# Norms beside self-attention: turning a norm one step later, normalizing ahead of the next deviation, and more dummy transposes at the start

## The chip, the cores and the metric

The kernel runs on one core of a Trainium2 chip. The metric is the device time of one execution in microseconds; below 1% this is about small differences, so the median of several runs counts. Beside the times there is a profile of one execution: the span of the core's instructions, and what each engine did in it. The engines are TensorE (PE, and PEld for its weight loads), VectorE (DVE), ScalarE (ACT), GpSimd (POOL) and SyncE (SP), which issues most DMAs.

## The reference

One transformer block in float32: two batches of 1024 tokens with 256 features, 16 heads of 64, a context of 154 tokens with 192 features.

```
h = layernorm(x, ln1);  x = attention(h, h, sa_*) + x
h = layernorm(x, ln2);  x = attention(h, ctx_768, ca_*) + x
h = layernorm(x, ln3);  p = h @ ff_w1 + ff_b1;  a, gate = halves of p
out = a * gelu(gate) @ ff_w2 + ff_b2 + x
```

`attention` projects queries, keys and values, takes softmax(q k / 8) v by head, and multiplies by an output matrix.

## The kernel before

The order of all instructions is written out by hand; each engine runs its own in that order. There are three stages: self-attention (about 20 to 720 us), cross-attention (to about 890 us) and the gated feed-forward part.

**Self-attention** goes over 16 units, a unit being one batch and one pair of heads. A unit has 8 steps (the loop over `p`), and a step handles 128 query rows of the pair's two heads against all 1024 keys. In step `p`:

- `self_first(p)`: TensorE makes scores into two PSUM tiles (line L544, tile `s`), VectorE takes their row maxima (L730), and after that ScalarE takes exponents (L555).
- `flush(stores)` stands between the scores and the exponents: it issues the copies out of PSUM that the step before left behind.
- `join(p - 1)`: the two halves of a row's keys lie on different partitions, so the maxima and sums are exchanged by four small DMAs (tile `st`). GpSimd takes differences (`dd`, L573), ScalarE their exponents (`ee`, L579), GpSimd denominators, VectorE reciprocals (`rd`), and GpSimd scales the exponents' rows (L668).
- `turn_group`: VectorE transposes scaled blocks for the value product (L693).
- Then one piece of other work for TensorE. The last step of each half unit does the first half of the value products (`po`, L596, into both banks of the pool `ps_o`), the first step of the next does the second half. Of the remaining steps, `run_work` fills each with a projection (`pq_sa`, `pk_sa` L387, `pv_sa` L423), or, where no projection is left, with output products (`py_sa`, L518).

`run_work(n, n_side, bank)` first does projections from the queue `work`, `n` banks' worth. It then does `n_side` entries of the queue `side`, then the deferred statistics (`slow`), and then output products from the queue `outs` for the banks that are left.

**Norms** are put into `side` by `norm_beside`, in steps that run beside the attention of other units. `norm_pieces` gives four kinds of pieces. `stats` are VectorE's `bn_stats` and `bn_aggr`. `deviation` is `var` (L265) and `rstd` (L269) on GpSimd. `normalize` is `off` on VectorE (L275) and two instructions that write the normalized tiles, on ScalarE (L294) or on GpSimd (L291). `turn` is four 128x128 transposes on TensorE (L304, tile `ph_ln`) into one bank, whose four copies with gain and shift on ScalarE (L319) or VectorE (L315) are left in `stores`. Which piece goes into which step is set by `lag`. For the narrow norms (ln1 of batch 1 and ln2 of batch 0, both beside self-attention) a step takes one token tile, and otherwise two. `run_work` gives `side` entries to steps 5 and 6 of a unit (counted from 0), so a narrow norm takes six units. A narrow norm's turn falls into step 5, which has a projection, and its normalize into step 6, which has output products.

**The start** (`warm`): while the first inputs are on their way, TensorE transposes the identity matrix (L1304), 12 times, then the context (L221), then 8 times. Next comes the transpose of the first gains and shifts (L1317), which waits for their DMA.

Of the kernel before, what the change touches and what calls it, by code (L numbers as in the profile page):

```python
# [18 lines left out]
def tile_transformer_block(ctx: ExitStack, tc: tile.TileContext, a: dict, out: bass.AP):  # L19
# [12 lines left out]
    NT = S // P  # L32
# [20 lines left out]
    SH = GH // 2  # L53
# [50 lines left out]
    for n in names:  # L104
        k = n_of[n]
# [82 lines left out]
    for n in names[2:]:  # L188
        own = rows[row_of[n] - n_cols:row_of[n] - n_cols + n_of[n], :]
        p = HR if n in twice else P  # L190
# [137 lines left out]
    def tile_order(kind):  # L328

        if kind == "ff":  # L330
            return list(range(NT))
        return [t for i in range(NT // 2) for t in (i, NT // 2 + i)]

    def narrow(kind, b):

        return kind == "sa" or kind == "ca" and b < B - 1

    def add_biases(kind, b):

        bo = {"sa": "sa_bo", "ca": "ca_bo", "ff": "ff_b2"}[kind]  # L340

        def add(t):
            xs = xt[b, t // GT][:, t % GT, :]
            nc.gpsimd.tensor_tensor(xs, xs, bias[bo], ALU.add)

        later.extend(lambda t=t: add(t) for t in range(NT))
        if b == B - 1 and kind != "ff":
            later.append(lambda: load_bias({"sa": "ca_bo", "ca": "ff_b2"}[kind]))

    def norm_beside(kind, b):  # L350

        after = {"sa": None, "ca": "sa", "ff": "ca"}[kind]
        stats, deviation, normalize, turn = norm_pieces(kind, b)
        n = 1 if narrow(kind, b) else 2
        lag = {}
        for fns, first in ((turn, 3), (stats, 0), (deviation, 1), (normalize, 2)):
            for i, fn in enumerate(fns):  # L360
                t = i if fns is stats else 2 * i + 1
                lag.setdefault(first + t // n, []).append((fn, fns is turn))
        for k in range(NT // n + 3):
            tiles = tile_order(kind)[k * n:(k + 1) * n]
            needs = [(after, b, half, t) for half in range(NQ) for t in tiles if after]

            def step(fns=lag[k]):
                slow.extend(fn for fn, _ in fns if fn in stats)
                done = [fn() for fn, _ in fns if fn not in stats]
                return next((fn for fn in done if fn), None)  # L370

            side.append((any(turns for _, turns in lag[k]), needs, step))
        if not narrow(kind, b):
            side.append((False, (), lambda: add_biases(kind, b)))

# [91 lines left out]
    def move_values(b, pr):  # L467

        v = unit_values(b, pr)
        for n in range(2):  # L470
            nc.sync.dma_start(
                out=held_v[n * QG:(n + 1) * QG, 3], in_=v[(1 - n) * QG:(2 - n) * QG])
# [132 lines left out]
    side, lates, slow = [], [], []  # L605
# [3 lines left out]
    def run(piece):  # L609
        done = piece()  # L610
        if done is not None:
            (adds if getattr(done, "adds", False) else stores).append(done)

    def flush(queue):
        for fn in queue:
            fn()
        queue.clear()

    def run_work(n, n_side, bank=None, n_sum=0):

        while n > 0 and work:
            n -= work[0].banks
            run(work.pop(0))
        for _ in range(min(n_side, len(side))):
            needs_bank, needs, fn = side[0]
            if needs_bank and not bank and n <= 0 or not added.issuperset(needs):
                break  # L630
            if needs_bank and not bank:
                n -= 1
            spare["bank"] = bank or mm_tile
            run(fn)
            side.pop(0)
        if not spare["turned"]:
            flush(slow)
        for i in range(min(max(n, 0) + n_sum, len(outs))):
            spare["out"] = mm_tile if i < n else sum_tile
            run(outs.pop(0))  # L640
# [8 lines left out]
    SA = 2 * SH * NU  # L649
# [35 lines left out]
    def turn_group(p, i):  # L685

        if p < 0:
            return
        h, g = divmod(p, SH)
        if g == 0 and i == 0:  # L690
            halves[h] = pt_.tile([P, 2 * NK, QH // 2], F32, tag="pT", name=f"pT_{h}")
        c = (2 * g + i) * KB
        nc.vector.transpose(  # L693
            halves[h][:, :, c:c + KB],
            slots[p]["p"][i].rearrange("p j (n k) -> p (j n) k", k=KB)
        )
# [25 lines left out]
    def self_first(p):  # L722

        b, pr = units[p // (2 * SH)]
        g = p % (2 * SH)
        q, k, _ = qk["sa", b, pr]
        st = small.tile([P, 2, 2, 2, 2], F32, tag="st8", name=f"st_{p}")
        sc = [scores(f"{p}_{i}", q, k, 2 * g + i) for i in range(2)]
        for i in range(2):
            nc.vector.tensor_reduce(st[:, 0, 0, i, :], sc[i], AX.X, ALU.max, negate=True)  # L730
            if i == 0:
                reciprocals(p - 2)

        def then():
            slots[p] = {"st": st, "p": [exponents(f"{p}_{i}", sc[i], st, i) for i in range(2)]}
            join(p - 1)
            exchange(st)

        return then
# [3 lines left out]
    def self_beside(ui):  # L743

        nxt = self_pieces(*units[ui + 1]) if ui + 1 < NU else cross_pieces(*units[0])
        if ui + 1 < NU:
            if ui % 2 == 0 and ui:
                work.append(value_piece(*units[ui], 1))
            work.extend(nxt)
            if ui == 0:  # L750
                work.append(unit_value_piece(*units[1], 0, GT))
            if ui % 2:
                work.append(value_piece(*units[ui + 1], 0))
        else:

            work.extend(nxt[:1])
            held.append(costing(2, lambda: cross_queries(*units[1], KB, tag="KT")))
            held.extend(nxt[1:])
        if ui >= HP:
            ob, og = divmod((ui - HP) // HP, NQ)  # L760
            t0 = (ui % HP) * 2
            out_pieces("sa", ob, og, out_order("sa")[t0:t0 + 2])
        if ui == 1:
            norm_beside("sa", 1)
        if ui in (4, 6):
            add_biases("sa", (ui - 4) // 2)
        if ui == NPAIR + 1:
            norm_beside("ca", 0)
# [507 lines left out]
    with tc.manual_schedule():  # L1276
        stats, deviation, normalize, turn = norm_pieces("sa", 0, True)
        spare["bank"] = sum_tile

        def emit(*pieces):  # L1280
            for piece in pieces:
                run(piece)
            flush(stores)
# [18 lines left out]
        def warm(n):  # L1302
            for _ in range(n):
                nc.tensor.transpose(own[0][:, 1, :P], ident, ident)  # L1304
# [7 lines left out]
        for turned in [turn_context(b) for b in range(B)]:  # L1312
            turned()
        spare["bank"] = sum_tile
        warm(8)
        emit(stats[0], stats[1], deviation[0], stats[2], normalize[0], stats[3], deviation[1])
        nc.tensor.transpose(own[1][:, 1, :n_cols], rows1, ident[:n_cols, :n_cols])  # L1317
        nc.scalar.copy(cols[:, :n_cols], own[1][:, 1, :n_cols])
# [33 lines left out]
        for p in range(SA):  # L1352
            if p % (2 * SH) == 0:
                self_beside(p // (2 * SH))
            if p == SA - SH:
                work.extend(held)
                held.clear()
            then = self_first(p)
            flush(stores)
            then()  # L1360
            turn_group(p - LAG - 1, 1)
            turn_group(p - LAG, 0)
            if adds:
                adds.pop(0)()
            flush(kept)
            if later and (p < 4 or p % (2 * SH) in (2, 4, 6)):
                later.pop(0)()
            if p in ahead:
                ahead[p]()
            load_ahead(p)  # L1370
            h, hg = divmod(p, SH)
            ui, n = divmod(p, 2 * SH)
            if h and hg == SH - 1:
                run(lambda: self_values(h - 1, 0))
            elif h > 1 and hg == 0:
                run(lambda: self_values(h - 2, 1))
            else:
                run_work(2 if p < SA - SH else 1, h % 2 or h == 0, sum_tile)
            if n == SH:
                move_values(*units[ui])  # L1380
            if hg == LAG:
                if n == SH + LAG and ui in (0, 1, NU - 1):

                    pr = {0: 2, 1: 4, NU - 1: 6}[ui]
                    run(lambda: context_keys(pr, sum_tile))
                    kept.append(context_keys(pr + 1, mm_tile))

        for c in range(CA):
# [13 lines left out]
            ui, n = divmod(c, len(CG))  # L1402
# [87 lines left out]
        for k in range(2 * FU):  # L1490
# [18 lines left out]
            while n_left > 0 and sums:  # L1509
                fn, n = sums.pop(0)  # L1510
# [51 lines left out]
```

## Time and profile before

| | |
|---|---|
| Runs | 1063.14, 1064.46, 1069.09 us; median 1064.46 |
| Profiled execution, its own time | 1065.06 us |
| Its span | 1063.3 us (1.8 lie around it) |
| Busy: TensorE, VectorE, GpSimd, ScalarE | 99%, 83%, 72%, 61% |
| DMA | 60.95 MB, mean 57 GB/s |

How to read it: a busy share says how long an engine had something in it, not that it set the time. The chain of waits is followed back from the last instruction and says which engine the end waited for at each moment. The page cuts the span into 40 slices of 26.6 us:

```profile
PE   8999999999999999999999999999999999999998
DVE  4799899998989989999989899979877887565554
ACT  4776677677766666666777766665666554343231
POOL 2677777778777787777777777777766876479984
```

TensorE is busy in nine tenths or more of nearly every slice. VectorE comes close to it in the self-attention stage.

### The profile page before, as it was taken

How to read it: one execution, taken by the hardware profiler on the slowest of the kernel's cores; microseconds unless marked ns; L12 is line 12 of the kernel's file. 1: busy time of each engine (PE TensorE's matmuls, PEld its weight loads, DVE VectorE, ACT ScalarE, POOL GpSimd, SP SyncE). 2: the span in 40 equal slices, each digit the busy share in tenths (PEclk: the TensorE clock that was granted, in tenths of full speed). 3: DMA queues.
4: the chain of work that ended last, by engine and by line, in shares of the span. 5: the costliest groups of instructions: out<-in, count | busy, mean ns of one | idle time of the engine just before them, and what ended most of it. 6: DMA issues, size and time to landing. Idle time of an engine off the chain costs nothing.

```text
span 1063.3 us, 48592 instructions
## 1 busy us (share of the span) xinstructions
PE 1054.3 (99%) x20190; PEld 703.4 (66%) x20190; DVE 883.4 (83%) x1321; ACT 650.5 (61%) x2104; POOL 770.9 (72%) x1644
## 2 busy tenths in 40 slices
PE   8999999999999999999999999999999999999998
PEld 6556657555555556656665655566866667888998
DVE  4799899998989989999989899979877887565554
ACT  4776677677766666666777766665666554343231
POOL 2677777778777787777777777777766876479984
PEclk9999999999999999999999999999999999999999
DMA  4121121131011111111111101116776545000000
GB/s 132 51 61 54 25 73 47 26 69 34 15 45 35 32 44 32 42 34 34 44 34 33 45 14 39 33 51 154 175 181 170 124 99 115 16 10 11 21 10 31
DMA packets 83573, 60.95 MB, mean 57 GB/s; under 512 B 30994, under 2 KB 71898, under 8 KB 83354
## 3 DMA queue, kind: packets, MB, share of 16 engines
q1 hardware_dynamic: 82405, 57.01, 22.3%
q8 instruction: 159, 2.61, 1.0%
q10 hardware_dynamic: 949, 0.84, 0.2%
q14 instruction: 60, 0.49, 0.2%
HBM read 27.91 MB, written 2.10 MB: 28 GB/s over the span
## 4 chain that ended last, share of the span: by engine, by line
PE 93%; DMA 2%; DVE 1%; POOL 1%; ACT 1%; SPq 1%; issue 1%; POOLq 0%; DVEq 0%; ACTq 0%
PE s L544 20%; PE po L596 20%; PE py_sa L518 5%; PE py_ca L518 5%; PE pq_sa L387 5%; PE pk_sa L387 5%; PE pq_ca L387 4%; PE pv_sa L423 4%; PE pb L1084 4%; PE poc L963 4%; PE pq L1229 4%; PE sc L883 3%; PE pa L1084 3%; PE pc L1084 3%; PE pf L1259 1%; PE ph_ln L304 1%
## 5 line engine op out<-in xcount | busy, mean ns | idle before, releaser
L668 POOL TENSOR_SCALAR p<-p,rd,ee 128x512 f32<-128x512 f32 x512 | 390.4, 768 | 88.7 <-DVE rd L658 87.5
L555 ACT ACTIVATE p<-s,st 128x512 f32<-128x512 f32 x512 | 344.9, 686 | 174.6 <-DVE st L730 168.3
L730 DVE TENSOR_REDUCE st<-s 128x2 f32<-128x1024 f32 x256 | 308.6, 1206 | 55.9 <-issue 23.5
L693 DVE STREAM_TRANSPOSE pT<-p 128x1024 f32<-128x1024 f32 x256 | 302.4, 1218 | 0.9 <-POOL p L668 0.9
L544 PE MATMUL s<-k_sa,q_sa 64*32 64x512 f32 x4096 | 255.9, 591 | 0.4 <-ACT p L555 0.4
L596 PE MATMUL po<-pT,held_v 64*32 64x256 f32 x8192 | 237.9, 376 | 0.0
L596 PEld LDWEIGHTS po<-pT,held_v 64*32 64x32 f32 x8192 | 177.1, 106 | 70.3 <-issue 27.8
L544 PEld LDWEIGHTS s<-k_sa,q_sa 64*32 64x32 f32 x4096 | 86.6, 106 | 94.7 <-issue 51.2
L900 ACT ACTIVATE p<-sc,neg 128x154 f32<-128x154 f32 x256 | 96.1, 404 | 74.9 <-DVE rden L908 70.8
L911 POOL TENSOR_SCALAR p<-p,rden 128x154 f32<-128x154 f32 x256 | 96.8, 398 | 47.5 <-DVE rden L908 42.1
L555 ACT ACTIVATION_READ_ACCUMULATOR p<-s,st 128x1 f32 x512 | 103.9, 203 | 0.0
L573 POOL TENSOR_TENSOR dd<-st 128x8 f32<-128x8 f32 x128 | 25.6, 200 | 68.9 <-DMA st<-st 68.3
L518 PE MATMUL py_ca<-ca_wo,o_ca 128*128 128x256 f32 x256 | 60.2, 383 | 0.0
L518 PE MATMUL py_sa<-sa_wo,o_sa 128*128 128x256 f32 x256 | 59.5, 386 | 0.0
L518 PEld LDWEIGHTS py_sa<-sa_wo,o_sa 128*128 128x128 f32 x256 | 47.3, 190 | 17.9 <-issue 5.0
L387 PE MATMUL pq_ca<-hT_ln,ca_wq 64*64 64x512 f32 (+1 forms) x576 | 58.9, 589 | 0.0
L387 PE MATMUL pq_sa<-hT_ln,sa_wq 64*32 64x512 f32 (+1 forms) x976 | 57.7, 587 | 0.7 <-ACT held_v L433 0.7
L889 DVE TENSOR_REDUCE neg<-sc 128x6 f32<-128x924 f32 (+1 forms) x48 | 47.7, 994 | 12.7 <-PE sc L883 12.7
L387 PE MATMUL pk_sa<-hT_ln,sa_wk 64*32 64x512 f32 x960 | 56.7, 590 | 0.0
L900 ACT ACTIVATION_READ_ACCUMULATOR p<-sc,neg 128x1 f32 x256 | 56.4, 220 | 0.0
L927 DVE STREAM_TRANSPOSE pT_ca<-p 128x480 f32<-128x480 f32 (+1 forms) x96 | 52.8, 585 | 0.8 <-POOL p L911 0.6
L518 PEld LDWEIGHTS py_ca<-ca_wo,o_ca 128*128 128x128 f32 x256 | 47.4, 190 | 8.2 <-issue 1.9
(164 smaller groups left out, 1475.4 us busy)
## 6 DMA issues: line engine op xcount, KB each, us to landing
wf<-pT_ca SPq DMA_DIRECT2D x128, 128.0 KB, 2.4
st<-st SPq DMA_DIRECT2D x512, 1.0 KB, 1.7
held_v<-held_v SPq DMA_DIRECT2D x32, 256.0 KB, 3.6
sa_wq<-in_L_xattn_sa_wq_dram SPq DMA_DIRECT2D x32, 128.0 KB, 3.1
sa_wk<-in_L_xattn_sa_wk_dram SPq DMA_DIRECT2D x32, 128.0 KB, 3.2
sa_wv<-in_L_xattn_sa_wv_dram SPq DMA_DIRECT2D x16, 256.0 KB, 4.5
ca_wq<-in_L_xattn_ca_wq_dram SPq DMA_DIRECT2D x32, 128.0 KB, 3.8
wf<-in_L_xattn_ff_w_dram SPq DMA_DIRECT2D x12, 256.0 KB, 4.4
```

What stands on the lines that cost most here:

```text
L387: nc.tensor.matmul(pq[r][f:f + m, at:at + n], lhsT=wt[own, c, f:f + m], rhs=h[own, c, t0:t0 + n], start=(c == 0), stop=(c == NH - 1), tile ...
L518: nc.tensor.matmul(py[:, e * D:(e + 1) * D], lhsT=o[:, i, (t + e) * P:(t + e + 1) * P], rhs=wo[kind][:, g * HP + i, :], start=(i == 0), st ...
L544: nc.tensor.matmul(sc[a4 * KB:(a4 + 1) * KB, j, :], lhsT=q[r, c:c + KB], rhs=k[r, h * HB:(h + 1) * HB], start=True, stop=True, tile_positi ...
L555: nc.scalar.activation(pr[:, j, :], sc[:, j, :], AF.Exp, bias=st[:, 0, 0, i, j:j + 1], accum_out=st[:, 0, 1, i, j:j + 1],)
L596: nc.tensor.matmul(po[a2][d:d + KB, :QH // 2], lhsT=v[e][r, t, d:d + KB], rhs=pT[r, d // DH * NK + n, :], start=(t == 0 and e == 0), stop= ...
L668: nc.gpsimd.tensor_scalar(pr[:, j, :], pr[:, j, :], own["rd"][:, c:c + 1], own["ee"][:, 0, c:c + 1], op0=ALU.mult, op1=ALU.mult,)
L693: nc.vector.transpose(halves[h][:, :, c:c + KB], slots[p]["p"][i].rearrange("p j (n k) -> p (j n) k", k=KB))
L730: nc.vector.tensor_reduce(st[:, 0, 0, i, :], sc[i], AX.X, ALU.max, negate=True)
L900: nc.scalar.activation(pr_[:, j, i, :T], sc[:, j, i * T:(i + 1) * T], AF.Exp, bias=neg[:, j, i:i + 1], accum_out=den[:, j, i:i + 1],)
L911: nc.gpsimd.tensor_scalar(pr_[:, j, i, :T], pr_[:, j, i, :T], rden[:, j, i:i + 1], 1.0, op0=ALU.mult, op1=ALU.mult,)
L927: nc.vector.transpose(pTc["ring"][:, ui % 3, :, j, t0 * KB:(t0 + nt) * KB].rearrange("p n (i q) -> p i n q", q=KB), pr_[:, j, :nt, :].rear ...
L1084: nc.tensor.matmul(into[:, :BT], lhsT=lhs, rhs=wh[pair][i], start=first, stop=True, skip_group_check=True)
```

## The change

1. In `norm_beside`, a turn of a narrow norm comes one entry of `side` later, so in step 6 (with output products) instead of step 5. The wide norms keep their place.
2. Within one entry, `normalize` now stands ahead of `deviation` of the following tiles. This moves something only where both run on GpSimd: ln2 of batch 1 and ln3 of batch 0.
3. In the self-attention loop, `run_work` is called twice: projections, deferred statistics and output products first, and then the entry of `side`. So a turn's transposes stand behind the output products of their step.
4. At the start, `warm(24)` stands for the second `warm(8)`.

In the built program TensorE has the 16 added transposes and the eight narrow turns in their new places. ScalarE has the eight groups of four copies one step later: behind the exponents of step 6, their factors and, in six of the eight, two normalizing activations, and ahead of the exponents of step 7. In each of these step 7s the first product into the second `po` bank has a wait on ScalarE that it did not have before. GpSimd has two normalizing instructions ahead of `var` and `rstd` six times. VectorE's and SyncE's orders stay as they were.

```diff
         lag = {}
-        for fns, first in ((turn, 3), (stats, 0), (deviation, 1), (normalize, 2)):
+        last = 4 if n == 1 else 3
+        for fns, first in ((turn, last), (stats, 0), (normalize, 2), (deviation, 1)):
             for i, fn in enumerate(fns):
                 t = i if fns is stats else 2 * i + 1
                 lag.setdefault(first + t // n, []).append((fn, fns is turn))
-        for k in range(NT // n + 3):
+        for k in range(NT // n + last):
...
-            def step(fns=lag[k]):
+            def step(fns=lag.get(k, [])):
...
-        warm(8)
+        warm(24)
...
             else:
-                run_work(2 if p < SA - SH else 1, h % 2 or h == 0, sum_tile)
+                run_work(2 if p < SA - SH else 1, 0)
+                run_work(0, h % 2 or h == 0, sum_tile)
```

More of the change, by code (lines that the diff above doesn't have):

```diff
@@ L370, in step @@
                 return next((fn for fn in done if fn), None)
-            side.append((any(turns for _, turns in lag[k]), needs, step))
+            side.append((any(turns for _, turns in lag.get(k, [])), needs, step))
         if not narrow(kind, b):
```

## The prediction

> **What bounds the kernel now.** I read the page first, its busy times and the chain that ended last; then the chain in order of time around the places that the change touches; then the waits; then the timeline of one such place, engine by engine.
>
> ```profile
> PE 1054.3 (99%) x20190; PEld 703.4 (66%) x20190; DVE 883.4 (83%) x1321; ACT 650.5 (61%) x2104; POOL 770.9 (72%) x1644
> PE 93%; DMA 2%; DVE 1%; POOL 1%; ACT 1%; SPq 1%; issue 1%; POOLq 0%; DVEq 0%; ACTq 0%
> ```
>
> TensorE is busy for 1054.3 us of the span and carries 93% of the chain. So in the self-attention stage whatever TensorE issues less, or waits more, goes into the time in full, and what VectorE, ScalarE or GpSimd do counts only where TensorE waits for it.
>
> Four transposes that turn a norm ("a turn") stand eight times in that stage: four for ln1 of batch 1 and four for ln2 of batch 0. Here are two units of eight steps in the chain, one with a turn and one without. The columns are start, length, what.
>
> ```profile
> 214.74 3.43 PE pk_sa L387 x64
> 218.18 0.59 PE ph_ln L304 x4
> 218.76 1.88 PE s L544 x32
> 220.64 3.65 PE py_sa L518 x16
> 384.42 3.43 PE pk_sa L387 x64
> 387.85 1.72 PE s L544 x32
> 389.57 3.65 PE py_sa L518 x16
> ```
>
> From the projection (pk) to the output products (py) it takes 220.64 - 214.74 = 5.90 us with the turn and 389.57 - 384.42 = 5.15 without. A turn costs 0.75 where it stands, between narrow tiled products (64x32) on both sides.
>
> **The turn moved: what TensorE saves.** The change takes each turn out of that place, its step 5 of 8, and puts it behind the output products of step 6, which are 128x128 like the transposes. Four transposes in a row cost their own pitch there.
>
> ```profile
> PEld ph_ln L304 <- ACT p L555: 5.0, 8, 0.8
> 389.50 3.32 PEld L518 LDWEIGHTS py_sa<-sa_wo,o_sa 128*128 128x128 f32 x16 [0.84 <-ACT k_sa L410]
> 598.27 0.66 PE L304 MATMUL ph_ln<-ident,hT_ln 128*128 128x128 f32 x4
> 600.74 3.72 PE L518 MATMUL py_sa<-sa_wo,o_sa 128*128 128x256 f32 x16
> 604.39 1.95 PE L544 MATMUL s<-k_sa,q_sa 64*32 64x512 f32 x32
> 606.13 3.66 PE L596 MATMUL po<-pT,held_v 64*32 64x256 f32 x128
> 609.58 1.92 PE L544 MATMUL s<-k_sa,q_sa 64*32 64x512 f32 x32
> L1304 PE MATMUL first<-ident x20: 272/417/473, 1.9 to 6.8; 128*128 128x128 f32 x20
> ```
>
> One transpose lasts 0.27 us (272 ns, the last row's minimum), so four in 0.66 have a pitch of (0.66 - 0.27) / 3 = 0.13, and a turn behind the output products adds 4 x 0.13 = 0.5. Taking away 0.75 and adding 0.5 leaves a gain of 0.25 a turn, 2.0 us over eight. The first row would promise more: the weight loads of the eight turns sat idle for 5.0 us "for ScalarE". I don't count that as a wait. The second row shows the same 0.84 idle before output products that follow narrow products without a turn: it is what the weight path shows at such a change of shape, and the chain's 0.75 holds it already.
>
> **The turn moved: the wait that it brings.** A turn writes into one of the two banks of ps_o, and four ScalarE activations (L319) empty it in the step after. Both banks are taken again by the value products po, at step 7. Now the turn is at step 5, its copies at step 6 and po at step 7. In the changed program the turn is at step 6, and its copies stand in ScalarE's queue in step 7, behind step 6's four exponents, their factors and the next pair's two normalizing activations (L294). The instruction order of the built program shows it: the second bank's first po product has a wait on ScalarE that it didn't have. TensorE issues in order, so all of po and the next scores queue behind it. When are the copies done? The turn of 598:
>
> ```profile
> 599.46 1.54 ACT L319 ACTIVATE hT_ln<-ph_ln,cols 128x128 f32<-128x128 f32 x4
> 600.11 1.22 DVE L730 TENSOR_REDUCE st<-s 128x2 f32<-128x1024 f32 x1 [1.22 <-ACT held_v L433]
> 600.57 0.72 POOL L269 TENSOR_TENSOR rstd_ln<-var_ln,power 128x2 f32<-128x2 f32 x1
> 601.52 1.52 POOL L668 TENSOR_SCALAR p<-p,rd,ee 128x512 f32<-128x512 f32 x2 [0.24 <-DVE rd L658]
> 602.45 2.36 DVE L693 STREAM_TRANSPOSE pT<-p 128x1024 f32<-128x1024 f32 x2
> 604.74 0.12 DVE L275 SCALAR_TENSOR_TENSOR off_ln<-mv_ln,rstd_ln 128x2 f32<-128x2 f32 x1
> 604.89 1.09 ACT L294 ACTIVATE hT_ln<-x,off_ln,rstd_ln 128x256 f32<-128x256 f32 x2 [0.63 <-DVE off_ln L275]
> 606.90 0.69 ACT L555 ACTIVATE p<-s,st 128x512 f32<-128x512 f32 x1 [0.92 <-DVE st L730]
> ```
>
> Normalizing ends at 604.89 + 1.09 = 605.98, 0.15 before po starts (606.13): were ScalarE no earlier than now, the copies would end at 605.9 + 1.54 = 607.4, some 1.3 behind po's present start. It gets earlier, because step 6's scores come 0.75 earlier. VectorE's reduction (600.11) sat idle for 1.22 before them and follows. GpSimd's scaling can't: its rstd ends at 600.57 + 0.72 = 601.29, so scaling starts 0.24 earlier at most and ends at 602.8. The second of VectorE's two block transposes needs it: 602.8 + 1.2 = 604.0, and off comes at 604.05, 0.7 earlier. Normalizing then ends at 605.3, the copies at 605.2 + 1.54 = 606.75. The second bank's po waits until then, though TensorE is there at 606.13 - 0.25 = 605.9. Against now po is late by 606.75 - 606.13 = 0.6, all inclusive. Nothing gives that back: after po the next scores start at once (606.13 + 3.45 = 609.58). The exponents behind the copies lose nothing, they start at 606.90 for VectorE's reduction.
>
> Six of the eight turns share their step with a normalize; I take five of them like this one. The first differs, and of the two without a normalize (the last of each norm) one is shown:
>
> ```profile
> 181.70 0.20 POOL L573 TENSOR_TENSOR dd<-st 128x8 f32<-128x8 f32 x1 [1.09 <-DMA st<-st]
> 182.41 1.08 ACT L294 ACTIVATE hT_ln<-x,off_ln,rstd_ln 128x256 f32<-128x256 f32 x2
> 183.54 1.72 PE L596 MATMUL po<-pT,held_v 64*32 64x256 f32 x56
> 646.46 0.22 ACT L579 ACTIVATE ee<-dd 128x8 f32<-128x8 f32 x1
> 648.55 1.72 PE L596 MATMUL po<-pT,held_v 64*32 64x256 f32 x56
> ```
>
> In the first, ScalarE's factors come behind GpSimd's dd, and that waits for a DMA (181.70) which an earlier TensorE doesn't hasten. Normalizing stays at 182.41, the copies end at 183.4 + 1.54 = 184.95, po is late by 184.95 - 183.54 = 1.4. At 646.46 + 0.22 + 1.54 = 648.2 the copies of the last turn are done before po (648.55 - 0.25 = 648.3): the gain of 0.25 stays. Sum: 5 x 0.6 + 1.4 - 2 x 0.25 = +3.9 us. Bounds for one turn with a normalize: 0.25 won where the copies come in time, 1.4 lost where nothing on ScalarE moves; I take 0.6 because the timeline of the turn at 598 leads there link by link.
>
> **Normalize ahead of the next deviation.** Where GpSimd normalizes (ln2 of batch 1, ln3 of batch 0), two xn instructions now stand ahead of the next var and rstd, six times. Elsewhere the two are on different engines, and no order changes. One of the six is on TensorE's path:
>
> ```profile
> 844.93 0.71 POOL L269 TENSOR_TENSOR rstd_ln<-var_ln,power 128x2 f32<-128x2 f32 x1
> 845.64 1.09 POOL L291 TENSOR_SCALAR xn_ln<-x,rstd_ln,off_ln 128x256 f32<-128x256 f32 x2
> 845.12 0.96 PE L883 MATMUL sc<-kT,q_ca 64*64 64x154 f32 x24
> 846.78 0.55 PE L304 MATMUL ph_ln<-ident,xn_ln 128*128 128x128 f32 x3 [0.21 <-POOL xn_ln L291]
> 847.16 1.68 PE L518 MATMUL py_ca<-ca_wo,o_ca 128*128 128x256 f32 x7
> 859.14 0.79 PE sc L883 x24
> ```
>
> The scores start at 845.12 and take 0.79 on the chain, a turn 0.59, so the output products could start at 846.50; they start at 847.16. With xn ahead by var and rstd, about 1.0, that 0.65 goes. The rstd, later by 1.1, is needed one step on. For the other five I take nothing: the waits name no other of these turns as held by xn. Bounds: 0 to -0.65 here. Taken: -0.6.
>
> **Twenty-four dummies for eight.**
>
> ```profile
> 1.91 2.82 PE L1304 MATMUL first<-ident 128*128 128x128 f32 x12 [1.91 <-POOL ident masks.py:199]
> 6.66 0.38 PE L1304 MATMUL first<-ident 128*128 128x128 f32 x2
> 8.52 0.20 PE L1317 MATMUL first<-ident,held_v 8*128 8x8 f32 x1 [1.47 <-DMA held_v<-in_L_xattn_ln_b_dram]
> ```
>
> TensorE idles for 1.47 until a DMA lets L1317 go. The pitch of the first twelve is (2.82 - 0.47) / 11 = 0.21, that of the last two 0.38 - 0.27 = 0.11: the clock has risen by then, and it outlives the idle time (turns before and after have 0.27 a transpose). Sixteen more at 0.11 are 1.75 us: the last starts near 8.5, and L1317 comes at 8.6 for 8.52. Cost +0.1. The Trainium skill ("TensorE: Matmul & The Clock Gate", Part 4: PE-mode transpose) says that transposes don't bring the clock up, as they don't count as busy the same way; the pitch in these rows speaks against it.
>
> Sum: +3.9 - 0.6 + 0.1 = +3.4 us. The profiled execution took 1065.06, 0.6 above the median of the runs; on the median the sum gives 1064.46 + 3.4 = 1067.9 us. A measurement of this kernel can tell about 0.5%, 5.3 us, from no change, so this lies inside it: no change to speak of, on the slow side. Its own range, with the five at 0.2 to 1.1, is 1065 to 1071.
>
> **Rivals.** *The copies come in time.* ScalarE and VectorE run ahead far enough, po doesn't wait, and the eight turns win 0.25 each: -2.0 - 0.6 + 0.1, 1062.0 us. For it: VectorE does idle ahead of the reduction. Against it: GpSimd's rstd leaves 0.24, and the copies need 1.3. *Every turn pays like the first.* If the DMA of the maxima, or GpSimd, holds ScalarE in all six, po is late by 1.4 each time: 6 x 1.4 - 0.5 - 0.5 = +7.4, 1071.9 us, slower. It decides where step 7's copies start later than po's present start less 0.15. For it: normalizing ends just 0.15 before po now, and the first turn shows such a DMA. Against it: in the turn at 598 the normalize waits 0.63 for VectorE, not for a DMA. *The dummies outlast the idle time.* If the added ones run at 0.21, they take 3.4 from 6.9 to 10.3, and L1317 with the first turn is late by 1.8: 1069.7 us. The page above gives this case by its rule. Against it stands the 0.11 of the last ones. That the change doesn't do what it says I rule out: all three edits show in the instruction order.
>
> **How the numbers follow.** Forecast 0.65, copies in time 0.15, every turn like the first 0.13, dummies 0.07. The range is 1063.0 to 1071.3: it takes in the forecast's own range, leaves out the first rival and the upper part of the second. Slower than 1069.8: a quarter of the forecast, the second rival, half the third, 0.33. Faster than 1059.1 needs more than any step here gives, 0.04. The rest is within 0.5%: 0.63.
>
> **What would show it.** Right: the waits list po behind ScalarE's L319, eight or six times, 0.5 to 1.5 each; ph follows py without idle time; TensorE passes from the scores at 845 to py with no wait for xn; L1317 at 8.5 to 8.7. Wrong: po with no gap at step 7 while step 5 is 0.75 shorter, or L1317 past 9.

## The result, and the profile after

The changed kernel takes 1071.42 us in the median of 12 runs (1068.49 to 1075.21), the kernel before 1066.5 in the median of 12 (1063.14 to 1069.09). The ratio is 1.0045 [1.0032, 1.0059]: slower by 4.8 us, with the interval from 3.4 to 6.3. That is within the 0.5% that the prediction called no change to speak of, on the slow side, though the interval reaches past it. The predicted 1067.9 is 3.5 us too low: 2.0 of that is the base, since 1064.46 was the median of three runs and twelve gave 1066.5, and 1.5 is the change. The median lies 0.1 above the upper end of the range.

The profiled execution of the changed kernel took 1074.59 us, its span 1072.8, one of the longer ones. The page gives busy time and the chain's shares by engine:

```profile
PE 1058.9 (99%) x20206; PEld 735.6 (69%) x20206; DVE 885.4 (83%) x1321; ACT 649.9 (61%) x2104; POOL 773.8 (72%) x1644
PE 78%; DMA 5%; POOL 4%; DVE 4%; SPq 3%; ACT 3%; issue 2%; POOLq 0%; ACTq 0%; DVEq 0%
```

TensorE still looks 99% busy, as before; that number hides the change. The chain doesn't: TensorE's share falls from 93% to 78%, because the path now leaves it for ScalarE and what ScalarE waits for. The waits of the stretch from 165 to 665 us (idle us, times, longest) say where:

```profile
PEld po L597 <- ACT hT_ln L319: 7.3, 8, 1.4
PEld py_sa L519 <- ACT held_v L434: 6.2, 6, 1.6
PE po L597 <- ACT hT_ln L319: 4.0, 6, 0.9
PE py_sa L519 <- ACT held_v L434: 1.1, 2, 0.7
```

Six times the matrix products of po stand still for the turn's copies (L319), and twice the output products for copies of a projection (L434). Lines from L377 on carry a number one higher than before. This is the turn of unit 13, the one that the prediction followed at 598, in the chain in order of time:

```profile
608.28 3.65 PE py_sa L519 x16
611.93 0.44 PE ph_ln L304 x4
612.37 0.24 PE s L545
612.60 0.02 issue
612.63 0.05 ACT hT_ln L294
...
613.13 0.58 ACT hT_ln L294
613.72 1.39 ACT hT_ln L319 x4
615.11 0.04 issue
615.16 3.44 PE po L597 x116
```

The chain goes from TensorE's scores to ScalarE's normalize (L294), on to the copies behind it (L319), and comes back to TensorE with the second bank of po. The timeline has the same place by engine:

```profile
612.63 1.09 ACT L294 ACTIVATE hT_ln<-x,off_ln,rstd_ln 128x256 f32<-128x256 f32 x2 [0.55 <-DVE off_ln L275]
613.63 1.48 ACT L319 ACTIVATE hT_ln<-ph_ln,cols 128x128 f32<-128x128 f32 x4
614.04 0.63 PE L597 MATMUL po<-pT,held_v 64*32 64x256 f32 x8
615.16 3.44 PE L597 MATMUL po<-pT,held_v 64*32 64x256 f32 x116 [0.49 <-ACT hT_ln L319]
```

The first bank's products begin at 614.04 and the second bank's at 615.16, when the copies end (613.63 + 1.48 = 615.11).

To see what that is worth I take the distance from the start of a step's last score product to that of the next step's. The first score products won't do as a mark: they can start while the products before them still run, and some steps have that and others not. Step 6 of unit 5 has it:

```profile
263.66 0.72 PE L545 MATMUL s<-k_sa,q_sa 64*32 64x512 f32 x2
263.85 0.38 PE L424 MATMUL pv_sa<-sa_wv,hT_ln 64*32 64x256 f32 x1
...
264.06 1.90 PE L545 MATMUL s<-k_sa,q_sa 64*32 64x512 f32 x28
```

A turn touches steps 5, 6 and 7 of its unit; these are the sums of the three, in us. The last column adds all eight before rounding. Units 6 and 14 hold the turns without a normalize beside them.

| Kernel | unit 3 | 4 | 5 | 6 | 11 | 12 | 13 | 14 | all |
|---|---|---|---|---|---|---|---|---|---|
| before | 16.62 | 16.60 | 16.62 | 16.60 | 16.62 | 16.60 | 16.62 | 16.60 | 132.9 |
| after | 17.47 | 17.79 | 18.59 | 16.28 | 18.20 | 17.31 | 17.42 | 16.28 | 139.4 |
| copies at once (below) | 16.31 | 16.28 | 16.31 | 16.29 | 16.59 | 16.28 | 16.31 | 16.28 | 130.6 |

By step, the eight units add up to 47.3, 44.2 and 41.4 in steps 5, 6 and 7 before, and to 41.3, 48.9 and 49.2 after. Step 7 takes 5.17 before in each unit; after, it takes 6.19 to 6.67 in the six with a normalize and 5.17 in the two others. The expectations below were written with distances between first score products: there the usual step 7 reads 5.19, and the six long ones 5.84 to 6.32.

Of the 9.5 us between the two profiled spans, 6.5 are in these steps. The rest is spread over other steps: single executions of either kernel differ by 6 us and more, and the profiled one of the changed kernel is 3.2 above its median.

The other two edits behaved as the text said, or nearly. GpSimd's normalize now starts at 854.34, ahead of the next rstd:

```profile
854.34 1.09 POOL L291 TENSOR_SCALAR xn_ln<-x,rstd_ln,off_ln 128x256 f32<-128x256 f32 x2
854.87 0.96 PE L884 MATMUL sc<-kT,q_ca 64*64 64x154 f32 x24
855.76 0.66 PE L304 MATMUL ph_ln<-ident,xn_ln 128*128 128x128 f32 x4
856.25 1.89 PE L519 MATMUL py_ca<-ca_wo,o_ca 128*128 128x256 f32 x8
```

From the scores to the output products it is 856.25 - 854.87 = 1.38 us, against 847.16 - 845.12 = 2.04 before: 0.66 won. At the start the 24 dummies cover the whole idle time:

```profile
5.56 3.46 PE L1305 MATMUL first<-ident 128*128 128x128 f32 x24
8.94 0.22 PE L1318 MATMUL first<-ident,held_v 8*128 8x8 f32 x1
```

The transpose of the first gains comes at 8.94 with no wait, 0.42 later than before (8.52).

### The profile page after: what moved, and what is told of

Same layout as the page of the kernel before. It is cut to its first block, busy times and chain, and to the rows that moved or that the text cites. A ratio compares the mean times of both kernels' runs of the same rounds, so it can differ in the third digit from the quotient of the medians.

```text
span 1072.8 us, 48627 instructions
## 1 busy us (share of the span) xinstructions
PE 1058.9 (99%) x20206; PEld 735.6 (69%) x20206; DVE 885.4 (83%) x1321; ACT 649.9 (61%) x2104; POOL 773.8 (72%) x1644
## 4 chain that ended last, share of the span: by engine, by line
PE 78%; DMA 5%; POOL 4%; DVE 4%; SPq 3%; ACT 3%; issue 2%; POOLq 0%; ACTq 0%; DVEq 0%
PE po L597 17%; PE s L545 14%; PE py_ca L519 5%; DMA st<-st 5%; PE pq_ca L388 5%; PE pq_sa L388 4%; PE pb L1085 4%; PE py_sa L519 4%; PE pk_sa L388 4%; PE poc L964 4%; PE pq L1230 4%; SPq L566 3%; PE pv_sa L424 3%; PE sc L884 3%; PE pa L1085 3%; PE pc L1085 2%
## 5 line engine op out<-in xcount | busy, mean ns | idle before, releaser
L545 PE MATMUL s<-k_sa,q_sa 64*32 64x512 f32 x4096 | 271.6, 590 | 0.6 <-ACT p L556 0.6
L597 PE MATMUL po<-pT,held_v 64*32 64x256 f32 x8192 | 248.8, 376 | 4.4 <-ACT hT_ln L319 4.0
L597 PEld LDWEIGHTS po<-pT,held_v 64*32 64x32 f32 x8192 | 183.1, 106 | 74.1 <-issue 20.3
L545 PEld LDWEIGHTS s<-k_sa,q_sa 64*32 64x32 f32 x4096 | 107.2, 106 | 82.7 <-issue 37.4
L519 PEld LDWEIGHTS py_sa<-sa_wo,o_sa 128*128 128x128 f32 x256 | 47.3, 190 | 19.2 <-ACT held_v L434 6.2
L424 PE MATMUL pv_sa<-sa_wv,hT_ln 64*32 64x256 f32 x1792 | 55.2, 376 | 0.0
```

Of the source, the lines that this page charges most:

```text
L424: nc.tensor.matmul(pv[r][f:f + KB, e * VC:(e + 1) * VC], lhsT=h[half, c, t0:t0 + KB], rhs=wt[half, c, :], start=(c == 0), stop=(c == NH - ...
L519: nc.tensor.matmul(py[:, e * D:(e + 1) * D], lhsT=o[:, i, (t + e) * P:(t + e + 1) * P], rhs=wo[kind][:, g * HP + i, :], start=(i == 0), st ...
L545: nc.tensor.matmul(sc[a4 * KB:(a4 + 1) * KB, j, :], lhsT=q[r, c:c + KB], rhs=k[r, h * HB:(h + 1) * HB], start=True, stop=True, tile_positi ...
L597: nc.tensor.matmul(po[a2][d:d + KB, :QH // 2], lhsT=v[e][r, t, d:d + KB], rhs=pT[r, d // DH * NK + n, :], start=(t == 0 and e == 0), stop= ...
```

## The experiments

Theory A: what the change loses is the wait of po for the turn's copies, which stand on ScalarE behind the normalize. Its rivals stand in the expectations.

**The turn's move alone.** Against the changed kernel:

```diff
-        for fns, first in ((turn, last), (stats, 0), (normalize, 2), (deviation, 1)):
+        for fns, first in ((turn, last), (stats, 0), (deviation, 1), (normalize, 2)):
...
-        warm(24)
+        warm(8)
```

> The kernel before with the turn moved alone (one step later, right behind the output products); normalize stands behind the next deviation and the second group of dummies is 8, as before. Theory A: the time is lost in the wait of the value products po for the turn's copies on ScalarE. Then nearly all of the loss is here: six step 7s of 5.8 to 6.3 us where 5.19 is usual, the waits list names po behind L319 eight times with about 7 us of idle weight loads, and the time is 4 to 6 us over before (ratio 1.0035 to 1.006). Rival B: the sixteen dummies or the order on GpSimd lose it; then this is within 1 us of before.

Measured: 1071.67 us, ratio 1.0052 [1.0033, 1.0072], and PEld's waits of po for L319 are 6.6 us. All of the loss that can be measured is in the turn's move.

**Everything but the turn's move.**

```diff
-        last = 4 if n == 1 else 3
+        last = 3
...
-                run_work(2 if p < SA - SH else 1, 0)
-                run_work(0, h % 2 or h == 0, sum_tile)
+                run_work(2 if p < SA - SH else 1, h % 2 or h == 0, sum_tile)
```

> The changed kernel with the turn back in step 5 and one run_work call; what stays of the change is normalize ahead of the next deviation and 24 dummies for 8. Theory A: the two edits nearly cancel (0.2 to 0.4 lost at the start, 0.5 to 0.65 won at the first turn of ln3), so -0.3 us against before, within the noise. Rival C (the dummies cost more than the profile shows, since they outlast the first DMA): 2 us or more over before.

Measured: 1064.79 us, ratio 0.9992 [0.9979, 1.0006]. The normalize's new order and the dummies together can't be told from nothing.

**The copies at once.** The turn stays where the change puts it, but its four copies are issued in the turn's own step, so on ScalarE they stand ahead of the normalize.

```diff
             def step(fns=lag.get(k, [])):
...
+                if n == 1:
+                    for fn, turns in fns:
+                        if fn not in stats:
+                            done = fn()
+                            if turns:
+                                done()
+                    return None
```

> The changed kernel with one thing different: in the eight narrow turns the four copies out of the turn's bank are issued at once behind its transposes, so that on ScalarE they stand ahead of the two normalizing activations and not behind them. TensorE's order is that of the changed kernel. Theory A: the copies end about 1.1 us earlier, the six long step 7s fall from 5.8-6.3 to 5.2-5.4 us, and the time falls by 3.5 to 5.5 us, to within 2 us of before. Rival B (the place of the transposes behind output products, or output products that wait for the emptying of the projection's banks, loses the time): step 6 stays above 6.2 us, step 7 hardly counts, and the time stays 3 us or more over before.

Measured: 1064.28 us, ratio 0.9982 [0.9971, 0.9993]: faster than both kernels. The waits, and the same turn of unit 13 (lines from there on are seven higher):

```profile
PEld po L604 <- ACT hT_ln L319: 1.4, 7, 0.2
```

```profile
603.02 1.50 ACT L319 ACTIVATE hT_ln<-ph_ln,cols 128x128 f32<-128x128 f32 x4 [0.69 <-PE ph_ln L304]
604.41 1.09 ACT L294 ACTIVATE hT_ln<-x,off_ln,rstd_ln 128x256 f32<-128x256 f32 x2
604.65 3.66 PE L604 MATMUL po<-pT,held_v 64*32 64x256 f32 x128
```

The copies end at 604.52, the normalize comes behind them, and po's 128 products run through in 3.66. Step 7 is back at 5.17 in seven of the eight units, and 5.45 in unit 11 (6.19 to 6.67 in the six turns with a normalize of the changed kernel). The table's last row is 2.2 below the kernel before: the move itself does win about 0.28 a turn, and what the change lost lay in the copies' place in ScalarE's queue.

**The turn ahead of the output products.** In step 6, but not behind them:

```diff
-                run_work(2 if p < SA - SH else 1, 0)
-                run_work(0, h % 2 or h == 0, sum_tile)
+                run_work(2 if p < SA - SH else 1, h % 2 or h == 0, sum_tile)
```

> The changed kernel with run_work called once as before, so that the turn, still in step 6, stands ahead of the output products and not right behind them. ScalarE's order is that of the changed kernel. Theory A: the copies stand at the same place in ScalarE's queue and po waits for them just as long; step 7 stays at 5.8 to 6.3 us and the time within 1 us of the changed kernel's. Rival B (the place right behind the output products is what costs): back to within 1.5 us of before.

Measured: 1071.98 us, ratio 1.0058 [1.0039, 1.0077]. The place beside the output products doesn't matter while po waits. The same edit on top of the copies at once, where po doesn't wait:

> The changed kernel with each narrow turn's copies issued in the turn's own step, and the turn ahead of the output products of step 6 instead of behind them. Theory A: the copies are far ahead of po in both, so no wait for them, ratio 0.997 to 0.999; what is left is the order on TensorE alone: a turn between scores and output products adds what the one behind output products adds, within 0.1 us each, so the two kernels differ by under 1 us. Rival (the place behind the output products is what wins the 0.25 a turn): 1 to 2 us slower than the same with the turn behind them.

Measured: 1063.33 us, ratio 0.9972 [0.9961, 0.9984], its eight units 131.0 in the table's sum, 0.04 a turn above the one with the turn behind. So what wins is step 6 with its output products, not the place behind them. This version and the two others with the copies at once are faster than both kernels, and can't be told from each other.

**The normalize a step earlier.** It comes in step 5, right ahead of its turn in step 6; the copies stay one step behind the turn.

```diff
-        for fns, first in ((turn, last), (stats, 0), (normalize, 2), (deviation, 1)):
+        for fns, first in ((turn, last), (stats, 0), (normalize, last - 1), (deviation, 1)):
```

> The changed kernel, copies again one step behind their turn, but each narrow norm's normalize one side step later, so in step 5, right ahead of its turn in step 6: no normalize stands ahead of the copies in step 7 any more. Theory A: without the normalize the copies end about 1.1 us earlier, like those of the last turn of each norm, which had none ahead; the waits of po for them fall from 7.3 us to under 2 and the time to 1064 to 1066, ratio 0.998 to 1.000. Rival D (the copies are late for the factors that they stand behind, not for the normalize): the waits stay at 4 us or more and the ratio at 1.003 to 1.005. Rival E (the turn then waits for its own normalize, which has just been issued): po is free, but the turn's transposes wait for ScalarE, by 0.5 us or more a turn, and the time stays near 1069.

Measured: 1070.07 us, ratio 1.0042 [1.0025, 1.0058]. The time that theory A gave was wrong, though po is free (step 7 is 5.17 in all eight units). Rival E's time came out, but not for its reason. The timeline of unit 13, steps 6 and 7:

```profile
602.46 1.09 ACT L294 ACTIVATE hT_ln<-x,off_ln,rstd_ln 128x256 f32<-128x256 f32 x2 [0.55 <-DVE off_ln L275]
603.46 1.17 ACT L434 COPY held_v<-pv_sa 128x256 f32<-128x256 f32 x4
604.40 3.72 PE L519 MATMUL py_sa<-sa_wo,o_sa 128*128 128x256 f32 x16 [1.13 <-ACT held_v L434]
607.96 0.60 PE L304 MATMUL ph_ln<-ident,hT_ln 128*128 128x128 f32 x4
...
610.23 3.66 PE L597 MATMUL po<-pT,held_v 64*32 64x256 f32 x128
```

The turn doesn't wait for its normalize. The output products ahead of it do: they need banks that step 5's projection filled, and the copies that empty those (L434, or L411 where the projection is pk) stand behind the normalize now. It is the same wait at another bank. Step 6 takes 6.57 to 7.16 in the eight units, where it takes 5.97 without a wait. So both places tried for the normalize ahead of a bank's copies cost that bank's next user.

**The normalize twice.** This adds a known dose: each normalizing activation of the narrow norms runs twice, the second writes the same values again.

```diff
-                    nc.scalar.activation(
-                        own, xs, AF.Identity, bias=off[:, i:i + 1], scale=rstd[:, i:i + 1])
+                    for _ in range(2 if narrow(kind, b) and not first else 1):
+                        nc.scalar.activation(
+                            own, xs, AF.Identity, bias=off[:, i:i + 1], scale=rstd[:, i:i + 1])
```

> The changed kernel with each normalizing activation of the narrow norms beside self-attention executed twice; the second one writes the same values again. That puts 1.1 us more of ScalarE ahead of the copies in each of the six steps 7 that have both. Theory A: po, which already waits there, is late by the whole 1.1 more, 6 x 1.1 = 6.6 us above the changed kernel, 1077 to 1079, ratio 1.010 to 1.012. Rival (what is lost is the order on TensorE, or the exchange by DMA, and the copies are only seen last): less than 2 us more, ratio under 1.0065.

Measured: 1081.23 us, ratio 1.0153 [1.0132, 1.0175], more than the theory gave. The eight units add up to 149.4, 10.0 above the changed kernel: 1.0 to 1.4 in units 3, 4, 12 and 13, nothing in 6 and 14, but 2.8 and 2.4 in units 5 and 11. Here is po's second bank in unit 3, and in unit 5 with the windows around it (in a window's row the number behind the five engines is the granted clock):

```profile
186.97 3.44 PE L598 MATMUL po<-pT,held_v 64*32 64x256 f32 x116 [1.65 <-ACT hT_ln L320]
```

```profile
277.50 5.13 PE L598 MATMUL po<-pT,held_v 64*32 64x256 f32 x116 [2.12 <-ACT hT_ln L320]
```

```profile
274.00:277.50 3.50, 1.39 (x32) 0.35 (x16) 3.23 (x4) 3.43 (x9) 3.23 (x7) 1.00 0.26 76
277.50:281.00 3.50, 3.50 (x74) 2.28 (x82) 2.04 (x3) 2.73 (x9) 1.56 (x5) 0.56 0.01 2
```

After 1.65 us of idle time the 116 products take 3.44; after 2.12 they take 5.13, with a granted clock of 0.56. Unit 11 has the same:

```profile
533.33 5.13 PE L598 MATMUL po<-pT,held_v 64*32 64x256 f32 x116 [2.00 <-ACT hT_ln L320]
```

Without these two losses of 5.13 - 3.44 = 1.69 the dose costs 10.0 - 3.4 = 6.6 us, and 6.6 was expected. Theory A's size holds in this execution, and a wait can have a price of its own. Its length alone doesn't decide that: unit 4 has the longest of these waits, and its products take 3.44 at a granted clock of 1.00.

```profile
232.02 3.44 PE L598 MATMUL po<-pT,held_v 64*32 64x256 f32 x116 [2.31 <-ACT hT_ln L320]
```

**The dummies.** The copies at once with 8 dummies for 24:

> The changed kernel with each narrow turn's copies issued in the turn's own step, and with 8 dummy transposes as before instead of 24. Theory A (the value products wait for copies that queue behind the normalize; the dummies cost the 0.4 us that the first gains' transpose came later, most of it made up within 30 us): 1063.5 to 1064.5, ratio 0.998, at most 0.4 us under the same with 24 dummies, and that transpose back at 8.5. Rival C (the added dummies are worth something behind the start, by an earlier clock): above the same with 24 dummies by 0.5 or more.

Measured: 1062.27 us, ratio 0.9978 [0.9964, 0.9991]; with 24 it was 0.9982. Neither theory is shown by the median. The profiled execution shows something else:

```profile
9.05 0.24 PE L1325 MATMUL first<-ident,held_v 8*128 8x8 f32 x1 [2.74 <-DMA held_v<-in_L_xattn_ln_b_dram]
```

```profile
8.00:10.00 2.00, 0.95 (x5) 0.96 (x6) 0.00 (x0) 0.17 (x1) 0.63 (x1) 0.59 0.61 134
10.00:12.00 2.00, 2.00 (x6) 1.14 (x4) 1.87 (x8) 1.29 (x3) 0.55 (x1) 0.50 0.92 245
```

The DMA came later than in the profile of the kernel before (9.05 for 8.52), TensorE idled 2.74, and worked at a clock near 0.5 until about 15 us. The mean granted clock of an execution tells whether the clock fell anywhere in it: it reads 0.996 to 0.998 in 22 of the 70 executions of the kernel before that ran beside the experiments, and 1.000 in all 60 of the kernels with 24 dummies told of so far, but for the one with the normalize twice, where all four read 0.996 or 0.997. In the kernel before, the executions with a lowered clock took 2.3 to 2.7 us more in the median than the others, in each of the three sets. Two more runs tested this; in the first, no second dummies at all, with the turn ahead and its copies at once:

```diff
-        warm(24)
```

> The turn ahead of the output products with its copies at once, as in the run before, but no second group of dummy transposes at the start at all (24 there). Theory F (TensorE falls to half pace when it idles for about 2 us while the first inputs come, as with 8 dummies in a third of the executions of the kernel before, whose granted clock then reads 0.996 to 0.998 and whose median is 2.4 us longer): the idle time ahead of the first gains' transpose is 2.5 us or more in nearly every execution, nearly all read 0.996 to 0.998 or stay at half pace from the start, and the median is 1.5 to 3 us above that of the same with 24, 1064.8 to 1066.3. Rival (the dummies do nothing but come in the way): 0 to 0.5 us under it, 1062.8 to 1063.3.

Measured: 1064.51 us, ratio 0.9993 [0.9978, 1.0009]; 7 of 12 executions read 0.997 or 0.998. In the profiled one the clock falls as well, behind a shorter idle time:

```profile
7.71 0.20 PE L1324 MATMUL first<-ident,held_v 8*128 8x8 f32 x1 [1.95 <-DMA held_v<-in_L_xattn_ln_b_dram]
```

```profile
10.00:12.00 2.00, 2.00 (x17) 1.78 (x18) 0.41 (x3) 0.43 (x1) 0.69 (x1) 0.50 0.69 194
```

The same with 24 had 0.9972 [0.9961, 0.9984]; the intervals overlap, and the two didn't run side by side, so the price of 1.5 to 3 isn't shown. Within this run the seven executions with the lower clock have a median of 1064.3 and the five others one of 1064.7, which shows no price either.

In the second, the kernel before with 24 for the second 8:

```diff
-        warm(8)
+        warm(24)
```

> The kernel before with 24 dummy transposes for the second 8 and nothing else. Theory F: the granted clock reads 1.000 in every execution; the median is that of the undisturbed executions of the kernel before plus up to 0.4 for the later first transpose, 1065.0 to 1065.5, ratio 0.999 to 1.000, and the spread is narrower. Rival (as predicted, 0.1 us lost and nothing won): ratio 1.000 to 1.001, with the same spread as the kernel before.

Measured: 1065.94 us (1063.69 to 1067.92), ratio 0.9999 [0.9986, 1.0011]. The clock is 1.000 in all 12, as theory F says, but the median is no better. The 17 of 23 executions of the kernel before beside it that read 1.000 have a median of 1065.1, against 1065.9 here. That would fit dummies that take away the lowered clock and make the undisturbed executions later, but the spread of single executions is too wide to show it. In the profile the first gains' transpose comes at 9.17 for 8.52.

## Why the prediction was right, and where it was off

- **The forecast case held.** Slower by a few us, with po waiting on ScalarE for the turn's copies: as written, and the run without that wait shows it to be the cause. The size of the change was forecast at +3.4, and measured at +4.8. Of the signs named, po waits in the six turns with a normalize (0.39 to 0.87 each, where 0.5 to 1.5 was named), the turn follows the output products without a gap, and the wait for xn is gone; the transpose of the first gains missed its 8.5 to 8.7 with 8.94.
- **The wait of po** is the term that was mis-sized most. Against step 7 of before, the prediction has 0.6 + 0.25 = 0.85 for five turns and 1.4 + 0.25 = 1.65 for the first, 5.9 in all. Step 7 is longer by 1.17 in the first and 1.02 to 1.50 in the other five, 7.8 in all, and 7.1 in the run with the turn's move alone. The prediction let the normalize start 0.7 earlier in five turns like the one at 598. Counted from step 5's last score product it starts 0.5 and 0.6 earlier in units 13 and 12, but only 0.1 earlier in unit 4, and 0.3 and 0.7 later in units 11 and 5. In these three GpSimd's rstd, which the prediction held where it was, ends 1.2 to 1.6 later, VectorE's second block transpose idles for the scaling behind it (0.36, 0.43 and 0.90), and off and the normalize queue behind that. In unit 5:

```profile
270.15 1.25 DVE L694 STREAM_TRANSPOSE pT<-p 128x1024 f32<-128x1024 f32 x1 [0.90 <-POOL p L669]
```

  The first turn went the other way: its normalize was to stay where a DMA put it, but it starts 0.5 earlier, because GpSimd's differences, which wait for that DMA, come 0.6 earlier: here the DMA did follow an earlier TensorE.
- **TensorE's gain of 0.25 a turn** is there: 0.28 a turn with the copies at once, and in the changed kernel the two turns without a normalize win 0.32 each. Steps 5 and 6 together were to shorten by 2.0 over the eight turns; they shorten by 1.3. What is missing is lost in units 5 and 11, whose step 6 takes 6.76 and 6.37 instead of 5.97, because there the output products wait as well. In the run with the turn's move alone the two steps shorten by 2.05. Unit 5 in the timeline:

```profile
265.04 0.20 POOL L574 TENSOR_TENSOR dd<-st 128x8 f32<-128x8 f32 x1 [1.67 <-DMA st<-st]
...
265.61 0.21 ACT L580 ACTIVATE ee<-dd 128x8 f32<-128x8 f32 x1 [1.46 <-POOL dd L575]
265.73 1.18 ACT L434 COPY held_v<-pv_sa 128x256 f32<-128x256 f32 x4
...
266.68 1.56 PE L519 MATMUL py_sa<-sa_wo,o_sa 128*128 128x256 f32 x6 [0.72 <-ACT held_v L434]
```

  The exchange by DMA is late, then GpSimd's differences, ScalarE's factors, the projection's copies behind them, and the output products. The prediction looked at what stands ahead of the turn's copies in step 7, and never at the copies of step 5's projection, which are under the same pressure once step 5 is 0.75 shorter. Here GpSimd's differences come 1.4 us behind the first of the step's score products (263.66); with the copies at once they came 0.9 ahead of it. Why the exchange is late just there stays open. The move of half a megabyte of held_v runs on the DMA queues at that time, but it does so in the other kernels too, and in the run with the turn's move alone unit 5's step 6 takes 5.97. No run was made without that move.
- **The last turn of each norm** was to win 0.25 and wins 0.32, in both norms: step 7 is untouched, as forecast.
- **"Every turn pays like the first"**, the second rival, had the right engine and too high a price for these steps: 6 x 1.4 - 0.5 = +7.9 forecast, +6.5 in this one execution. In four of its six turns the DMA (unit 3) or GpSimd (units 4, 5 and 11) does hold ScalarE, as it said, and these four lose 0.85 to 1.97; the two like the turn at 598 lose 0.7 and 0.8. So the profiled execution lies between the forecast's 0.6 a turn and the rival's 1.4.
- **"The copies come in time"** fell in the changed kernel. With the copies put in time the ratio is 0.9982 [0.9971, 0.9993], 1.9 us won with an interval from 0.7 to 3.1; the rival's sum was -2.4.
- **The normalize on GpSimd** won 0.66 where 0.65 was forecast, link by link.
- **The dummies** were forecast at +0.1 and cost 0.4 at that place in this profile. In the changed kernel they take 3.46, which is neither 24 x 0.11 = 2.6 nor 24 x 0.21 = 5.0: the granted clock there rises at 6.9, within the 24. The eight profiles with 24 have the transpose at 8.26, 8.36, 8.47, 8.94, 9.04, 9.07, 9.17 and 9.24. The first three are those in which the clock had risen before the 24 began, which then take 2.79, and they are not later than before (8.52). The third rival's 10.3 was not reached, but four are past the 9 that was named as a sign against the forecast. What the forecast lacked is that the moment at which the clock rises, and the idle time that the dummies fill, differ from one execution to the next.
- **The nearness of the number.** The median of the changed kernel came 3.5 above the forecast, and 2.0 of that is the base. The two mis-sized terms don't cancel; in the profiled execution both err to the same side, by 1.9 and 0.7.

## What to carry to other kernels

When a step is moved that leaves a PSUM bank to be emptied, follow the emptying instructions in their engine's queue, not only the step: what stands ahead of them there is what the bank's next user waits for, and the order of two ScalarE jobs of 1.1 and 1.5 us made the difference between 1.0045 and 0.9982 here. A gain that TensorE makes by itself has to be checked against every copy whose deadline moves forward with it, in the steps before the one in question too. And a busy share of 99% says nothing of such a wait; the chain and the list of waits do. Distances between steps are best taken between marks that don't overlap the step before: counted between first score products, the waits of po would have seemed 2.2 us smaller in sum and TensorE's gain would have seemed lost.

## What the runs showed of the hardware that was not expected

- The clock can fall after a shorter idle time than I had thought. Idle times of 1.95, 2.00, 2.12 and 2.74 us were each followed by a granted clock near 0.5 for 3 to 7 us; 1.47 and 1.65 were not, but neither was one of 2.31. The Trainium skill ("TensorE: Matmul & The Clock Gate", Part 1) gives one idle window of about 3.4 us for this; the four values here are all below that, and decide.
- What sets the 2.31 apart may be its place in time. In the trace with the normalize twice the changes of the granted clock (up at 4.85, down at 277.92, up at 281.33, down at 533.92) lie whole multiples of 3.41 us apart. With that grid drawn through every trace that records the clock, the four stretches ahead of a fall hold 1.95 to 2.12 us of idle time. Once the clock is up, no other stretch holds more than 1.89: that one is part of the 2.31 us (229.72 to 232.02), which a border of the grid cuts at 230.13. No run moved an idle time against the grid, so this stays an inference from four falls.
- A step's first score products can start while the last products before them still run, up to 0.5 us ahead. With the same instruction order, step 6 with a turn seems to take 5.94 us in some units and 6.2 to 6.3 in others when it is counted between first score products. In the first kind the step's scores last 1.92 us from the first start to the last end, in the second 2.2 to 2.3. Counted between last score products it takes 5.97 in all eight units with the copies at once. Why some units have this lead and others not stays open.
